# A sparse attention layer on one core: three pairs of tiles and a single one, turned by VectorE instead of TensorE, and slots cleared behind the sort

## The chip, the cores and the metric

The kernel runs on one core of a Trainium2 chip. The metric is the device time of one execution in microseconds. The engines are TensorE (PE, with its weight loads as PEld), VectorE (DVE), ScalarE (ACT), GpSimd (POOL) and SyncE (SP, which here only issues DMAs). GpSimd issues the indirect DMAs: gathers and scatters by a list of row numbers.

## The reference

```python
# x: (2708, 1024) f32; adj: (2708, 2708) f32 of zeros and ones, about 0.15% ones; W_q, W_k, W_v: (1024, 1024)
h = maximum(layernorm(x), 0)
q, k, v = h @ W_q.T + b_q, h @ W_k.T + b_k, h @ W_v.T + b_v
z = (q @ k.T) / sqrt(1024) * adj
z = where(z == 0, -10000, z)
out = x + relu(softmax(z, axis=1) @ v)
```

## The kernel before

A row of `adj` has a handful of ones, so the kernel never forms the full `z`. It finds each row's neighbours (at most 16), sorts the rows by their number of neighbours, and from then on works on 22 tiles of 128 sorted rows. `W_q` and `W_k` are multiplied into one matrix, so a score is a product of a transformed row `q` with a neighbour's row of `h`; and the weighted sum over neighbours' rows of `h` (the row `u`) is taken before `W_v` is applied. So there are two large products, each over 21 tiles or so: `q` from `h`, and the output `o` from `u`.

**Units.** The loop `for n, unit in enumerate(units)` (L1225) runs over 20 units: ten q pairs, (0,1) to (18,19), and ten o pairs in the order in which the attention finishes tiles; the last one is (16,9), and tile 8 comes alone behind them (`alone`). A unit multiplies a pair of tiles (256 rows) by a 1024x1024 matrix by Strassen's scheme in Winograd's form (`multiply`, L1044): seven block products instead of eight, each of four 128x512 steps in fp32, in banks `ps0`, `ps1` and `psy`. Between them `after(0)` to `after(6)` emit what other engines do meanwhile. The unit `FIRST` = 4 is pair (8,9), and `FIRST + 1` is the sixth, (10,11).

**Operands.** TensorE needs the tiles transposed. `blocks` (L711) makes the operands of the next unit: `a11`, `a12` from the first tile, `a22`, `s3` from the second, and their sums `s1` to `s4`. There are two ways. Either TensorE turns a tile in eight transposes of 128x128 (`half_turned`, L415; results in `pt`, copied by ScalarE, L718), or the tile arrives so that VectorE's transpose of 32x32 blocks suffices (`faces`, L705): ScalarE copies `u` with its columns in another order into `v` (L944), `v` is stored in `u_dram`, and SP loads it back by quarter rows (`by_quarters`, L700). A tile of the second kind stands in `faced_tiles`. Which tiles of o pairs are such is decided in `sums` when `u` is complete, by how far ahead of its unit that is:

```python
if now < [unit - 2, 2] and unit <= len(q_pairs) + 4:
    faced_tiles.add(t)
```

Of the q pairs none was such: the first eight tiles are taken as they come, the others are gathered whole from `h_dram` by GpSimd (`gather`, L612, tiles `qr_...`).

**The sort.** It is in two halves. Tiles 8 to 21 are sorted first, their table being stored in `tab_dram1` and loaded back. Tiles 0 to 7 (`EARLY`) are sorted in unit 4: VectorE finds the last keys, TensorE counts them (`ps_in`, `ps_all`, L678 and L680), VectorE makes the positions `pos_i` (L689), GpSimd puts the rows to `tab_dram0` in eight indirect DMAs (L626) and loads the table. Behind that it gathers `pq_6` and the first slots `g0` on, and the attention's stream begins.

**The attention.** Eleven slots `g0` to `g10` of 128x1024 (and two in `M`) hold neighbours' rows. Per slot VectorE makes a score (L863) and later a weighted addition to `u` (L923). This stream is advanced by `advance(share)` beside the products, 20.9 us a unit, less 2.3 us for each faced tile that VectorE has to turn. VectorE's order is as written (`manual_schedule`) from unit 4 on; the other engines' order is made by a scheduler. The slots are cleared once before the stream: eight on VectorE in front of the sort (L1254), three on GpSimd behind the counts (L1304).

**Outputs.** When an o pair is done, ScalarE applies relu to `y`, GpSimd adds rows of `x` by an indirect DMA that accumulates (`add_x`, L1109) and scatters `y` to the output (`scatter`, L808), each scatter standing behind the next add (`send`, L1168). The last pair goes through `ends` (L1140), the single tile through L1355 to L1371.

Of the kernel before, what the change touches and what calls it, by code (L numbers as in the profile page):

```python
# [10 lines left out]
FT = mybir.dt.float32  # L11
# [54 lines left out]
def tile_preln_masked_attention(  # L66
# [93 lines left out]
    pos_i = const.tile([P, NT], U32, name="pos_i")  # L160
    rows_i = whole[:, 0:NT]
# [488 lines left out]

    sorting, entered, sorted_at = [], [], []
# [267 lines left out]
    def sums(t):  # L919
# [20 lines left out]
        if now < [unit - 2, 2] and unit <= len(q_pairs) + 4:  # L940
            faced_tiles.add(t)
        if t in faced_tiles:
# [168 lines left out]
    def o_results(ta, tb):  # L1111
# [12 lines left out]
        def c12(Z, u2):  # L1124
# [5 lines left out]
            send(add_x(ya, ta))  # L1130
            sent.append((ya, ta))

        def c21(Y):
            nc.scalar.activation(yb[:, lo], Y, AF.Relu)  # L1134
            send(add_x(yb, tb))
            sent.append((yb, tb))
# [29 lines left out]
    sent = []  # L1166

    def send(behind):  # L1168

        while sent:  # L1170
            y, t = sent.pop(0)
            with tc.issue_after(behind.ins):
                scatter(y, t, P)

    def tail(t):
        n = tiles[t][1]
        y = work.tile([P, D], FT, tag="q", name=f"y_{t}", bufs=4)
        nc.sync.dma_start(y[:n], tail_dram.to_broadcast([n, D]))
        add_x(y, t, n)
        scatter(y, t, n)  # L1180
# [44 lines left out]
    for n, unit in enumerate(units):  # L1225
# [7 lines left out]
        share = 20.9 / 7  # L1233
# [5 lines left out]
        def after(i):  # L1239
            now[1] = i  # L1240
            if (n, i) in steps_ahead:
                follow(steps_ahead[n, i])
            if (n, i) == (2, 5):
                owe(8)
                owe(9)
                rows_of[FIRST] = load_rows(units[FIRST])
                owe(10)
                owe(6)
                owe(7)
                rows_of[FIRST + 1] = load_rows(units[FIRST + 1])  # L1250
                pooled.close()
            if (n, i) == (FIRST, 1):
                for g in slots[:HIGH - 3]:
                    nc.vector.memset(g, 0.0)  # L1254
# [23 lines left out]
            if nxt is not None:  # L1278

                if i == (3 if n == 0 else 4 if turn else 0):  # L1280
                    ops_of[n + 1] = blocks(*rows_of[n + 1], nc.gpsimd if n + 1 < FIRST - 1 else None)
                    with tc.issue_after(products[-1].ins) if n + 1 == FIRST else nullcontext():
# [18 lines left out]
            if (n, i) == (3, 5):  # L1301
                for s in range(8, HIGH):
                    for c in range(0, D, D // 4):
                        clear = nc.gpsimd.memset(slots[s][:, c:c + D // 4], 0.0)  # L1304
                        tc.add_manual_dep(clear.ins, counted_at[-1].ins.name,
                                          mybir.DependencyInfo(mybir.DependencyClass.Sync, mybir.DependencyReason.DATA),
                                          reason="not beside the counts")
            if i == 3 and units[n - 1][0] == "o" and NT - 2 in units[n - 1][1:]:
                tail(NT - 1)
            if nxt is None and i == 1:  # L1310
                while alone not in done:
                    advance(1.0)
                r, = load_rows(("o", alone))
                single["turned"] = turned(r, "alone")
# [240 lines left out]
```

## Time and profile before

| | |
|---|---|
| time, median of 3 runs | 639.91 us (639.73 to 640.34) |
| time of the profiled execution | 639.94 us |
| its span, first to last instruction | 638.1 us |
| granted TensorE clock, mean | 0.997 |
| busy: PE / DVE / ACT / POOL | 98% / 82% / 44% / 56% of the span |
| transposes on TensorE, L415 | 273 ns each |

A row of a group reads: line, engine, operation, output<-input, shape and count, then busy time in us, mean ns of one, and the idle time in front of them with what ended it. A row of a timeline reads: start and length in us, engine, line, operation, and in brackets the idle time in front and what ended it. A DMA row gives the size and the median time from issue to landing.

### The profile page before, as it was taken

Reading aid. Unit: us, or ns where it says so; the run is one execution under the profiler, and the core shown is the slowest. Engines: PE = TensorE matmul, PEld = TensorE weight load, DVE = VectorE, ACT = ScalarE, POOL = GpSimd, SP = SyncE. Lnnn points to the kernel's source line nnn. Section 1 sums busy time; section 2 is a strip of 40 time slices with the busy share of each in tenths; the row PEclk is TensorE's granted clock in tenths of the full one; section 3 lists DMA queues with packets and bytes.
Section 4 is the critical chain, followed back from the end, with each engine's and each line's share of the span. In section 5 each row is a group of like instructions: output and inputs, shape, how many; then the busy total and the mean of one; then the engine's idle time right before and its main releaser. Section 6 shows DMA issues by size and latency. Waiting matters only on the chain.

```text
span 638.1 us, 6156 instructions
## 1 busy us (share of the span) xinstructions
PE 627.8 (98%) x1651; PEld 317.9 (50%) x1651; DVE 522.4 (82%) x1016; ACT 283.6 (44%) x423; POOL 360.2 (56%) x383
## 2 busy tenths in 40 slices
PE   9999999999999999999999999999999999999994
PEld 5777766444444444444444444444444444444441
DVE  5999888997997625999888999999999889989121
ACT  3538985849667533424342144343342432333200
POOL 2639960885768357565651663476466878633311
PEclk9999999999999999999999999999999999999998
DMA  8999997598796439996798998999999999853631
GB/s 335 407 362 321 342 351 286 200 323 330 255 379 231 171 95 317 327 323 223 233 299 289 290 414 222 295 344 311 363 382 325 325 290 291 266 145 77 187 119 50
DMA packets 60192, 176.96 MB, mean 277 GB/s; under 512 B 9799, under 2 KB 15255, under 8 KB 59512
## 3 DMA queue, kind: packets, MB, share of 16 engines
q0 software_dynamic: 25136, 78.41, 39.4%
q1 hardware_dynamic: 29514, 78.61, 35.0%
q10 hardware_dynamic: 5502, 19.48, 7.8%
q8 instruction: 15, 0.25, 0.2%
q14 instruction: 25, 0.20, 0.1%
HBM read 145.65 MB, written 40.74 MB: 292 GB/s over the span
## 4 chain that ended last, share of the span: by engine, by line
PE 90%; issue 4%; POOL 2%; DMA 2%; DVE 1%; POOLq 0%; ACT 0%; ACTq 0%; DVEq 0%
PE ps L1010 40%; PE psy L1010 29%; PE ps_y L476 6%; PE ps_x L476 4%; PE ps_z L476 4%; PE pt L415 4%; POOL g L610 2%; DMA v_dram<-u 1%; DMA M<-h_dram,tab 1%; PE ps_y L511 1%; DVE junk L863 0%; PE ps_h L1218 0%; PE ps_v L594 0%; DVE u L923 0%; DVE s L722 0%
## 5 line engine op out<-in xcount | busy, mean ns | idle before, releaser
L610 POOL DMA_INDIRECT g<-h_dram,tab x94 | 120.2, 1278 | 79.9 <-DVE u L923 30.0
L1010 PE MATMUL psy<-wlow,s 128*128 128x512 f32 x320 | 144.0, 592 | 0.0
L1010 PE MATMUL ps<-M,a 128*128 128x512 f32 x320 | 144.0, 593 | 0.0
L863 DVE SCALAR_TENSOR_TENSOR junk<-g,pq 128x1024 uint8<-128x1024 f32 x93 | 113.8, 1224 | 13.4 <-DMA g<-h_dram,tab 10.4
L1010 PEld LDWEIGHTS ps<-M,a 128*128 128x128 f32 x320 | 59.7, 190 | 70.4 <-issue 69.1
L923 DVE SCALAR_TENSOR_TENSOR u<-g,coef,u 128x1024 f32<-128x1024 f32 x69 | 88.4, 1281 | 7.0 <-ACT u L912 5.8
L1010 PEld LDWEIGHTS psy<-wlow,s 128*128 128x128 f32 x320 | 59.6, 190 | 69.2 <-issue 69.0
L389 DVE FIND_INDEX8 at<-ones,adj 128x8 uint32<-128x685 f32 (+1 forms) x88 | 74.5, 864 | 0.0
L1010 PE MATMUL ps<-wlow,s 128*128 128x512 f32 x160 | 72.0, 593 | 0.4 <-DVE s L722 0.4
L1010 PE MATMUL ps<-M,s 128*128 128x512 f32 x160 | 72.1, 592 | 0.0
L1010 PE MATMUL psy<-wlow,a 128*128 128x512 f32 x160 | 72.0, 593 | 0.0
L368 ACT ACTIVATE sized<-adj 128x2708 uint8<-128x2708 f32 (+1 forms) x22 | 54.3, 2467 | 7.4 <-DMA adj<-in_adj_dram 6.1
L298 POOL TENSOR_TENSOR hsum<-hsum,x 128x256 f32<-128x256 f32 (+1 forms) x56 | 38.6, 732 | 26.2 <-DVE wlow L444 22.5
L1109 POOL DMA_INDIRECT y<-in_x_dram,tab x19 | 34.2, 1798 | 28.9 <-ACT y L1134 12.1
L1010 PEld LDWEIGHTS ps<-wlow,s 128*128 128x128 f32 x160 | 30.3, 190 | 38.9 <-issue 38.5
L1010 PEld LDWEIGHTS psy<-wlow,a 128*128 128x128 f32 x160 | 30.3, 190 | 38.5 <-issue 37.3
L1010 PEld LDWEIGHTS ps<-M,s 128*128 128x128 f32 x160 | 30.3, 190 | 38.1 <-issue 37.4
L808 POOL DMA_INDIRECT out_dram<-y,tab x21 | 27.4, 1306 | 32.0 <-DMA y<-in_x_dram,tab 15.8
L912 ACT ACTIVATE u<-g,coef 128x1024 f32<-128x1024 f32 x18 | 20.7, 1149 | 35.8 <-DVE coef L911 35.6
L276 ACT ACTIVATE x<-x,r 128x1024 f32<-128x1024 f32 (+1 forms) x22 | 25.9, 1232 | 6.6 <-POOL r L266 6.6
L722 DVE TENSOR_TENSOR s<-a,pt 128x512 f32<-128x512 f32 x30 | 19.2, 681 | 10.9 <-ACT a L718 10.9
L476 PE MATMUL ps_y<-wlow 128*128 128x512 f32 x64 | 27.6, 592 | 0.0
(251 smaller groups left out, 843.3 us busy)
## 6 DMA issues: line engine op xcount, KB each, us to landing
adj<-in_adj_dram SPq DMA_DIRECT2D x21, 1354.0 KB, 11.5
x<-in_x_dram SPq DMA_DIRECT2D x21, 512.0 KB, 8.2
h_dram<-x ACTq DMA_DIRECT2D x21, 512.0 KB, 7.4
q_late<-q SPq DMA_DIRECT2D x12, 512.0 KB, 5.1
pq<-q_late SPq DMA_DIRECT2D x12, 512.0 KB, 6.6
u_dram<-v ACTq DMA_DIRECT2D x10, 512.0 KB, 6.4
or<-u_dram SPq DMA_DIRECT2D x40, 128.0 KB, 7.0
M<-in_wv_dram SPq DMA_DIRECT2D x4, 1024.0 KB, 8.4
```

Of the source, the lines that this page charges most:

```text
L276: nc.scalar.activation(xs[i][:n], xs[i][:n], AF.Relu, bias=r[:n, 4, i:i + 1], scale=r[:n, 3, i:i + 1])
L298: small.append(nc.gpsimd.tensor_add(hsum[:n, cols], hsum[:n, cols], xt[:n, cols]))
L368: nc.scalar.activation(sized[:n], a[:n, :, :PW], AF.Abs, accum_out=total[:n, t:t + 1])
L389: nc.vector.max_index(at[:n, k - first_k, g, :], ones[:n, 0:8], a[:n, g, :])
L415: nc.tensor.transpose(pt[:, c, :], xt[:, k * P:(k + 1) * P], ident)
L476: mm = nc.tensor.matmul(bank, a_tile(o + H * a[0], a[1], i), b(o), start=first and o == 0, stop=(o == H - 1), skip_group_check=True)
L610: return nc.gpsimd.indirect_dma_start(out=dst, out_offset=None, in_=src, in_offset=off, bounds_check=N - 1, oob_is_err=False)
L808: to = nc.gpsimd.indirect_dma_start(out=out, out_offset=bass.IndirectOffsetOnAxis(ap=ptab.bitcast(U32)[:n, t, SLOTS:SLOTS + 1], axis=0), i ...
L863: chained(lambda: nc.vector.scalar_tensor_tensor(junk, g_of[t][s], 1.0, tq[t], op0=ALU.mult, op1=ALU.mult, accum_out=zall[:, t, s:s + 1]))
L923: chained(lambda: nc.vector.scalar_tensor_tensor(u, g_of[t][s], coef[:, s:s + 1], u, op0=ALU.mult, op1=ALU.add))
L1010: mm = nc.tensor.matmul(bank, a[:, c, :], b[:, c, :], start=False, stop=(c == 3), skip_group_check=True)
L1109: return nc.gpsimd.indirect_dma_start(out=y[:n], out_offset=None, in_=x, in_offset=off, compute_op=ALU.add)
```

## The change

Five tiles more are turned by VectorE. For the sixth q pair (10,11), unit 5, GpSimd makes a list of quarter rows: `load_parts` loads the pair's row numbers from `tab_dram1` in four small DMAs into `part_i`, one operation turns them into numbers of quarter rows (4 x row + quarter), and `gather_parts` gathers each tile in four indirect DMAs of 128x256. The tiles of the last o pair (16 and 9) and the single tile 8 become faced tiles: `v`, a store, four quarter loads, transposes on VectorE (tile 8 in one of 128x1024). The eight slots that VectorE clears are cleared behind the sort, in three groups; the three on GpSimd behind the puts. An add of `x` is issued some steps later than its tile is done, and a scatter one add later still. From unit 15 on `share` is 21.5 us.

```diff
+    def load_parts(t):
+        src = tab_dram[1][(t - EARLY) * P:(t - EARLY + 2) * P, SLOTS:SLOTS + 1].bitcast(U32).rearrange("(m r) w -> r m w", r=QP)
+        for a in range(QUADS):
+            load = nc.gpsimd.dma_start(part_i[a * QP:(a + 1) * QP, :].unsqueeze(2), src)
...
+    def gather_parts(dst, i):
+        faced.append(dst)
+        for g in range(QUADS):
+            off = bass.IndirectOffsetOnAxis(ap=part_i[:, i * QUADS + g:i * QUADS + g + 1], axis=0)
+            cols = slice(g * D // QUADS, (g + 1) * D // QUADS)
+            nc.gpsimd.indirect_dma_start(out=dst[:, cols], out_offset=None, in_offset=off,
+                                         in_=h_dram.rearrange("n (a w) -> (n a) w", a=QUADS))
...
-        if now < [unit - 2, 2] and unit <= len(q_pairs) + 4:
+        if now < [unit - 2, 2] and unit <= len(q_pairs) + 4 or unit >= len(units) - 1:
             faced_tiles.add(t)
...
-            send(add_x(ya, ta))
-            sent.append((ya, ta))
+            due.append((now[0], 5, ya, ta))
...
-            send(add_x(yb, tb))
-            sent.append((yb, tb))
+            due.append((now[0] + 1, 1, yb, tb))
...
+    def add_due():
+        while due and due[0][:2] <= tuple(now):
+            y, t = due.pop(0)[2:]
+            send(add_x(y, t), 1)
+            sent.append((y, t, P))
...
-        share = 20.9 / 7
+        share = (20.9 if n < len(units) - 5 else 21.5) / 7
...
                 rows_of[FIRST] = load_rows(units[FIRST])
+                load_parts(units[FIRST + 1][1])
                 owe(10)
                 owe(6)
                 owe(7)
-                rows_of[FIRST + 1] = load_rows(units[FIRST + 1])
+                nc.gpsimd.tensor_scalar(part_i, part_i, float(QUADS), quarter[:, 0:1], op0=ALU.mult, op1=ALU.add)
+                rows_of[FIRST + 1] = [row_tile(f"qr_{t}") for t in units[FIRST + 1][1:]]
+                for i, r in enumerate(rows_of[FIRST + 1]):
+                    gather_parts(r, i)
                 pooled.close()
-            if (n, i) == (FIRST, 1):
-                for g in slots[:HIGH - 3]:
-                    nc.vector.memset(g, 0.0)
+            if n == FIRST and i in (1, 4, 5):
+                for g in slots[:4] if i == 1 else slots[4:6] if i == 4 else slots[6:8]:
+                    with tc.issue_after(sorted_at[-1].ins):
+                        nc.vector.memset(g, 0.0)
...
-            if (n, i) == (3, 5):
+            if (n, i) == (3, 6):
                 for s in range(8, HIGH):
                     for c in range(0, D, D // 4):
+                        with tc.issue_after(entered[-1].ins):
+                            nc.gpsimd.memset(slots[s][:, c:c + D // 4], 0.0)
...
             if nxt is None and i == 1:
+                uT = work.tile([P, D], FT, tag="hT", name="T_alone", bufs=2).rearrange("p (c q) -> p c q", q=P)
+                faces(uT, single["rows"], 0, DC)
+                single["turned"] = uT
+            if n == len(units) - 2 and i == 6:
                 while alone not in done:
                     advance(1.0)
-                r, = load_rows(("o", alone))
-                single["turned"] = turned(r, "alone")
+                single["rows"], = load_rows(("o", alone))
```

The order on TensorE in unit 4, around the counting of the sort, before (the names without their numbers are the operands above; `qr_10` and `qr_11` are the sixth pair's tiles):

```order
L1010 MATMUL psy_1332<-wlow_171,a22_1237 128x512 x4
L1010 MATMUL psy_1482<-wlow_171,s2_1435 128x512
L678 LDWEIGHTS before_86
L678 MATMUL ps_in_1497<-sort_1454,before_86 128x144
L680 LDWEIGHTS ones_h_84
L680 MATMUL ps_all_1499<-sort_1454,ones_h_84 128x144
L415 MATMUL pt_1536<-ident_75,qr_10_1313 128x128 x4
L415 MATMUL pt_1543<-ident_75,qr_10_1313 128x128 x4
L1010 MATMUL psy_1482<-wlow_171,s2_1435 128x512 x3
L415 MATMUL pt_1564<-ident_75,qr_11_1315 128x128 x4
```

and the same place after the change:

```order
L1034 MATMUL psy_1358<-wlow_177,a22_1243 128x512 x4
L701 LDWEIGHTS before_86
L701 MATMUL ps_in_1512<-sort_1481,before_86 128x144
L703 LDWEIGHTS ones_h_84
L703 MATMUL ps_all_1514<-sort_1481,ones_h_84 128x144
L1034 MATMUL psy_1497<-wlow_177,s2_1462 128x512 x4
L1034 MATMUL ps0_1401<-M_154,a12_1424 128x512 x4
```

The transposes of `qr_10` and `qr_11` are gone, and the counting stands one step of `s2` sooner. In the same way the eight transposes of `u_16`, of `u_9` and of `u_8` go from units 18 and 19; nothing else moves on TensorE.

The order on GpSimd between the last q gathers and the attention's first gather, before (`hsum` are additions for another sum, `tab_dram0` takes the puts):

```order
L612 DMA qr_9_1299<-h_dram_63,tab_97 128x1024
L298 TENSOR_TENSOR hsum_73<-hsum_73,x_10_1123 128x256 x4
L298 TENSOR_TENSOR hsum_73<-hsum_73,x_6_944 128x256 x4
L298 TENSOR_TENSOR hsum_73<-hsum_73,x_7_946 128x256 x4
L612 DMA qr_10_1313<-h_dram_63,tab_97 128x1024
L612 DMA qr_11_1315<-h_dram_63,tab_97 128x1024
L612 DMA qr_12_1584<-h_dram_63,tab_97 128x1024
L612 DMA qr_13_1586<-h_dram_63,tab_97 128x1024
L1304 MEMSET g8_1411 128x256 x4
L1304 MEMSET g9_1412 128x256 x4
L1304 MEMSET g10_1413 128x256 x4
L626 DMA tab_dram0_70<-tab_97,pos_i_109 1024x18 x8
```

and after it:

```order
L659 DMA part_i_115<-tab_dram1_71 32x8x1 x4
L302 TENSOR_TENSOR hsum_73<-hsum_73,x_10_1129 128x256 x4
L302 TENSOR_TENSOR hsum_73<-hsum_73,x_6_950 128x256 x4
L302 TENSOR_TENSOR hsum_73<-hsum_73,x_7_952 128x256 x4
L1280 TENSOR_SCALAR part_i_115<-part_i_115,quarter_110 128x8
L671 DMA qr_10_1324<-h_dram_63,part_i_115 128x256 x4
L671 DMA qr_11_1325<-h_dram_63,part_i_115 128x256 x4
L616 DMA qr_12_1588<-h_dram_63,tab_97 128x1024
L616 DMA qr_13_1590<-h_dram_63,tab_97 128x1024
L630 DMA tab_dram0_70<-tab_97,pos_i_109 1024x18 x8
L1339 MEMSET g8_1438 128x256 x4
L1339 MEMSET g9_1439 128x256 x4
```

Ten DMAs and one small operation are added ahead of the puts, and the clears have moved behind them.

The order on VectorE behind the sort after the change (the rows without MEMSET and STREAM_TRANSPOSE stood there before as well, `pt` being read in place of `s3`):

```order
L712 COPY pos_i_109<-deg_98 128x8
L728 STREAM_TRANSPOSE a11_1563<-qr_10_1324 128x4x4x32
L728 STREAM_TRANSPOSE a12_1565<-qr_10_1324 128x4x4x32
L1288 MEMSET g0_1430 128x1024
L1288 MEMSET g1_1431 128x1024
L1288 MEMSET g2_1432 128x1024
L1288 MEMSET g3_1433 128x1024
L728 STREAM_TRANSPOSE a22_1577<-qr_11_1325 128x4x4x32
L728 STREAM_TRANSPOSE s3_1579<-qr_11_1325 128x4x4x32
L745 TENSOR_TENSOR s1_1581<-a22_1577,s3_1579 128x512
```

Four clears stand between the two tiles' transposes; the other four follow in pairs behind `q_8` and `q_9`.

29 lines of the change are left out of this document (17 added, 12 removed).

## The prediction

> **What bounds the kernel now.** I read the page first. Its busy times (us, share of the span, instructions):
>
> ```profile
> PE 627.8 (98%) x1651; PEld 317.9 (50%) x1651; DVE 522.4 (82%) x1016; ACT 283.6 (44%) x423; POOL 360.2 (56%) x383
> ```
>
> And its chain of the work that ended last, by engine:
>
> ```profile
> PE 90%; issue 4%; POOL 2%; DMA 2%; DVE 1%; POOLq 0%; ACT 0%; ACTq 0%; DVEq 0%
> ```
>
> TensorE is busy for 98% of the span and carries 90% of the chain. VectorE is the next busiest, at 82%. The view of TensorE's waits (line waited for, total us, times, longest) says how little could be gained by feeding it better:
>
> ```profile
> PE ps_y L511 <- POOL hsum L121: 1.2, 1, 1.2
> PE ps L1010 <- DVE s L722: 0.4, 1, 0.4
> ```
>
> The first is in the prologue, which the change leaves alone. The second is one hole in TensorE's timeline, in front of a product's `s1` block:
>
> ```profile
> 389.03 3.67 PE L1010 MATMUL ps<-wlow,s 128*128 128x512 f32 x8 [0.36 <-DVE s L722]
> ```
>
> So TensorE's own work sets the time, and work taken off it shortens the kernel one for one as long as VectorE still delivers its operands. The groups view (busy us, mean ns) and the pieces of the chain (start, us; the first and the last of the five that go) price the work that the change removes:
>
> ```profile
> L415 PE MATMUL pt<-ident,qr 128*128 128x128 f32 x96 | 12.4, 273 | 0.0
> ```
>
> ```profile
> 217.48 0.87 PE pt L415 x8
> ```
>
> ```profile
> 597.38 0.87 PE pt L415 x8
> ```
>
> One 128x128 transpose reads 273 ns, but they overlap; a tile's eight advance the chain by 0.87 us.
>
> **The change part by part.** *Transposes off TensorE.* Five tiles lose their eight: qr_10 and qr_11 (the first at 217.48), u_16 and u_9 (in the last pair but one's product), u_8 (597.38). Nothing takes their place on TensorE. 5 x 0.87 = 4.4 us; unrounded starts in the timeline give 4.37. By the fifth pair's end TensorE is 1.75 us ahead, by the last pair 3.5, by the single tile 4.37.
>
> *The same turns on VectorE.* The row of an operand that comes as quarter rows already:
>
> ```profile
> L705 DVE STREAM_TRANSPOSE a<-or 128x512 f32<-128x512 f32 x15 | 10.0, 694 | 1.0 <-DMA or<-u_dram 1.0
> ```
>
> A pair costs four transposes, 4 x 0.69 = 2.8 us, and its four additions stay. The single tile costs one of 128x1024, an estimate of 1.4 us from two of 128x512. That is 2.8 + 2.8 + 1.4 = 7.0 us more on VectorE. The Trainium skill, page "VectorE: DVE Perf Modes", section "Rules for kernel authors", speaks against this: a 128x128 transpose belongs on TensorE if it may land in PSUM. The trace agrees as far as the engine's own time goes (0.87 us a tile there, 1.4 on VectorE). It disagrees on what that is worth: one engine carries 90% of the chain, the other 1%. What the 7.0 us do where VectorE is the bound is a rival below.
>
> *The sixth pair's trip.* GpSimd now issues four small loads `part_i`, one small multiply-add, and eight quarter gathers in place of two whole ones. Its queue before, in the timeline:
>
> ```profile
> 194.48 8.25 POOL L298 TENSOR_TENSOR hsum<-hsum,x 128x256 f32<-128x256 f32 x12
> ...
> 206.62 0.93 POOL L612 DMA_INDIRECT qr<-h_dram,tab  x1 [0.30 <-issue]
> 217.37 3.13 POOL L1304 MEMSET g<- 128x256 f32 x12 [9.82 <-ACT q L1099]
> 220.68 1.02 POOL L626 DMA_INDIRECT tab_dram<-tab,pos_i  x1 [0.18 <-issue]
> ...
> 235.20 0.98 POOL L612 DMA_INDIRECT pq<-q_dram,tab  x1 [4.45 <-DMA tab<-tab_dram]
> ```
>
> ```profile
> L642 POOL DMA_DIRECT2D tab<-tab_dram x1 | 0.6, 601 | 0.0
> ...
> tab<-tab_dram POOLq DMA_DIRECT2D x1, 2.2 KB, 6.7
> ```
>
> The last `qr` gather ended at 207.55 and GpSimd then idled 9.82 us. Added: 4 x 0.60 = 2.4, some 0.2 for the multiply-add, and six more gathers of 0.94 + 0.30 = 7.4, together 10.0: it ends at 217.6. The small loads land about 6.7 us after their issue, behind which 8.25 us of additions stand anyway, so the gathers don't wait. A part of the queue that was idle is now full, with 2 us or so to spare. The tile is turned around 220 and first multiplied near 230, so a landing of some 7 us is covered.
>
> *The start of the stream.* VectorE's timeline around the sort, and where it later waits for TensorE:
>
> ```profile
> 219.82 0.17 DVE L689 CAST pos_i<-deg 128x8 uint32<-128x8 f32 x1
> 224.75 1.28 DVE L722 TENSOR_TENSOR s<-a,pt 128x512 f32<-128x512 f32 x2 [4.75 <-ACT a L718]
> ...
> 241.99 1.23 DVE L863 SCALAR_TENSOR_TENSOR junk<-g,pq 128x1024 uint8<-128x1024 f32 x1 [7.25 <-DMA g<-h_dram,tab]
> ...
> 333.57 0.69 DVE L1094 TENSOR_TENSOR q<-ps,u 128x512 f32<-128x512 f32 x1 [1.05 <-PE ps L1010]
> ```
>
> ```profile
> L1254 DVE MEMSET g<- 128x1024 f32 x8 | 7.3, 912 | 1.3 <-issue 1.1 <-DVE q L1094 0.2
> ```
>
> The eight clears (7.3 us) go behind the sort, into the idle stretch that holds the 4.75 and the 7.25 us above: 12.0 us, against 7.3 + 2.8 = 10.1 put there. The sort is then limited by TensorE's counting matmuls rather than by the clears, and `pos_i` comes 0 to 1 us sooner. GpSimd's three clears (3.13 us) go behind the eight puts, into the 4.45 us in which it waits for the sorted table. So the puts begin at 219.3 to 220.2 instead of 220.68, and the first score falls 0.5 to 1.4 us earlier. TensorE is 1.75 us earlier. The difference, 0.35 to 1.25 us, is what VectorE falls behind in relation to TensorE; the wait of 1.05 us at 333.57 shows that it still stood ahead by that much there. I take it that nothing is left of the difference, and that the hole at 389 stays at 0.4 us (0 to 1.2).
>
> *The end.* Each turned tile now takes a trip: a copy on ScalarE, a store, four quarter loads, the transposes. The rows: when `u_9` and `u_8` were complete on VectorE (the first and third), when TensorE wants the single tile, and the pieces of the trip.
>
> ```profile
> 558.72 2.60 DVE L923 SCALAR_TENSOR_TENSOR u<-g,coef,u 128x1024 f32<-128x1024 f32 x2
> ...
> 574.59 5.25 DVE L923 SCALAR_TENSOR_TENSOR u<-g,coef,u 128x1024 f32<-128x1024 f32 x4 [1.66 <-ACT u L912]
> ...
> 586.70 1.28 DVE L929 SCALAR_TENSOR_TENSOR u<-g,m,u 64x1024 f32<-64x1024 f32 x1
> ...
> 605.16 0.69 DVE L1146 SCALAR_TENSOR_TENSOR y<-ps,y 128x512 f32<-128x512 f32 x1 [13.22 <-PE ps L1010]
> ```
>
> ```profile
> 611.82 3.60 PE L1010 MATMUL ps<-M,T_alone 128*128 128x512 f32 x8
> ```
>
> ```profile
> L944 ACT COPY v<-u 128x1024 f32<-128x1024 f32 x10 | 10.5, 1046 | 22.6 <-DVE u L923 20.7 <-DMA g<-h_dram,tab 1.8
> ```
>
> ```profile
> u_dram<-v ACTq DMA_DIRECT2D x10, 512.0 KB, 6.4
> or<-u_dram SPq DMA_DIRECT2D x40, 128.0 KB, 7.0
> ```
>
> ```profile
> DMA to landing us min/median/max: 3.0/6.9/15.1
> ```
>
> `u_9` was complete at 561.3; with copy 1.05, store 6.4, issues 1.5 and load 7.0 it is back at 577.3, and VectorE reaches its transposes after three of the adds that began at 574.59 and two transposes more, near 579.5: about 2 us spare (both shift alike with the stream). The single tile is tighter. `u_8` was complete at 588.0. It comes 0.5 to 1.4 earlier with the stream and 2.5 later for the transposes ahead of it: 589.1 to 590.0. Copy 1.05, store 6.4, four quarter loads issued within some 1.5 us and landing in 7.0, transpose 1.4: 606.4 to 607.4 by the medians. Those medians come from a stretch of heavier traffic; with 5 us for each transfer it is 603.0 to 604.0. I take 605. TensorE wants it at 611.82 - 4.37 = 607.45. VectorE's 13.22 us of idleness takes the 1.4. So the cover is about 2.5 us, and may be nothing.
>
> *Adds and scatters later.* Each scatter now stands behind the next tile's add. No chain piece holds an output store before the end, the row buffers are seven, and GpSimd is busy for 56%; I cost it at nothing, up to 1 us where a ScalarE write waits for a landed scatter.
>
> **Sum.** 639.94 (the profiled execution) - 4.37 = 635.57; the median of the runs shown lies 0.03 lower, so 635.5. If the 0.4 us hole goes too, 635.1.
>
> **The rivals.** *Slower: tile 8's trip through DRAM is late.* It replaces transposes that read u_8 in place. If the quarter loads land in the 15.1 us that the slowest took, T_alone is ready at about 615, TensorE waits 7.5 us in front of its first T_alone product, and the time is 643.0. It costs anything from 607.45 on, and makes the kernel slower than before from 611.82 on, which takes both transfers at 18 us together instead of 13.4. For it: a serial chain of copy, store, loads and transpose within 18 us, at the least forgiving place. Against: traffic is thinning out there. Chance 0.18 of a stall of any size, most of it 0.5 to 3 us (636 to 638.5); 0.04 of it above 639.94 + 0.2%.
>
> *The stream starts late.* GpSimd's indirect issues take 0.94 us in the quiet stretch quoted above, but over the stream:
>
> ```profile
> L610 POOL DMA_INDIRECT g<-h_dram,tab x94 | 120.2, 1278 | 79.9 <-DVE u L923 30.0 <-ACT u L912 25.2 <-issue 18.3
> ```
>
> At 1.28 the ten gathers take 3.4 us more, the puts start at about 221 to 221.5, the first score shifts to 242.5 where TensorE is 1.75 earlier, and VectorE is 2.2 us behind it; less the 1.05 us that it waited there, the hole at 389 grows by 1.2, and by 2 if `s1` of the next pair is late as well: 636.7 to 637.5. The Trainium skill, page "SBUF — State Buffer", section "SBUF: two separate sides", has a cause: VectorE's two-port operations keep GpSimd from writing descriptors. The quiet gather of 0.93 us at 206.62 stands in the stretch in question, with VectorE at work beside it, so I give this case 0.14.
>
> *VectorE becomes the bound.* It is 82% busy on the whole. If its 7.0 us came on the path whole, the time would be 639.94 - 4.37 + 7.0 = 642.6. The Trainium skill's rule on transposes, quoted above, points to this case. Against it: 12 us of waits at the sort and 13 us at the end have room for all three turns. 0.04.
>
> *The transposes were hidden anyway,* and the time stays at 639.9. The chain runs through all five pieces and TensorE shows no wait behind them: 0.02.
>
> **How the numbers follow.** The forecast has the remaining 0.62. About 0.2% (1.3 us) is what a measurement of this kernel can tell from no change. Faster by more: 0.62, 0.11 of the late tile, 0.12 of the late stream, 0.85. Within: 0.03 + 0.01 + 0.02 = 0.06. Slower: 0.04 + 0.01 + 0.04 = 0.09. The range begins at 634.9, the filled hole with its spread, and reaches to 638.3, which takes in the late stream and most stalls of the late tile.
>
> **What would show it.** Right: 40 fewer matmuls in the groups on TensorE, its busy time near 623.4; L415 on no chain piece in the three places; puts starting near 220 and a first score near 241; no wait on T_alone. Wrong: a wait of TensorE for the transpose of `or_8` (late tile); puts later than 221 and larger waits for `s` from 389 on (late stream); VectorE without idle time at the sort or at 592 to 605 (bound moved).

## The result, and the profile after

The changed kernel takes 7087.17 us (median of 6 runs, 7085.40 to 7093.04); the kernel before takes 640.12 us beside it (6 runs, 639.63 to 642.51). That is 11.07 times as long, with an interval of 11.055 to 11.082. The profiled execution took 7085.67 us.

The first lines of the page of after, its two largest groups, and TensorE's largest waits:

```profile
span 7083.9 us, 25332 instructions
PE 4431.3 (63%) x8515; PEld 1830.2 (26%) x8515; DVE 1235.9 (17%) x2766; ACT 351.0 (5%) x478; POOL 367.8 (5%) x394
```

```profile
L1527 PE MATMUL g_u<-g_hk,g_pT 128*128 128x512 f32 (+1 forms) x1936 | 1646.3, 998 | 1471.8 <-DMA g_hk<-h_dram 1471.8
L1508 PE MATMUL g_ps<-hT_all,g_qT 128*128 128x512 f32 (+1 forms) x2112 | 814.3, 545 | 0.0
```

```profile
PE g_u L1527 <- DMA g_hk<-h_dram: 1471.8, 462, 3.5
PE g_q L1489 <- DMA g_m<-m_dram: 704.3, 176, 4.9
```

TensorE has 8515 matmuls where it had 1651. The added ones write tiles named `g_...`, at lines from 1426 on, of which the trace of before has none. They belong to a second, general way of computing the layer: dense attention over all rows, in the block behind `with tc.If(some > 0)` (L1412). It is there for inputs that the sparse way can't hold, and `some` is a flag that the kernel computes. TensorE's timeline around that point, and the windows to either side of it (us; busy time and count of PE, PEld, DVE, ACT, POOL; granted clock; DMA share; GB/s):

```profile
608.34 3.60 PE L1034 MATMUL ps<-M,T_alone 128*128 128x512 f32 x8
...
615.20 0.28 PE L1380 MATMUL ps_f<-many,ones 128*128 128x1 f32 x2
615.34 3.68 PE L1034 MATMUL ps<-wlow,T_alone 128*128 128x512 f32 x8
618.86 7.03 PE L1034 MATMUL ps<-M,T_alone 128*128 128x512 f32 x16
635.56 2.07 PE L1426 MATMUL g_pm<-gk,gq 128*128 128x512 f32 x2 [9.67 <-DMA gk<-in_wk_dram]
```

```profile
0.00:633.00 633.00, 623.92 (x1611) 313.92 (x1611) 530.44 (x1039) 283.28 (x418) 367.81 (x394) 1.00 0.85 285
633.00:7084.00 6451.00, 3807.35 (x6904) 1516.28 (x6904) 705.43 (x1727) 67.72 (x60) 0.00 (x0) 0.71 0.19 67
```

The kernel runs as the prediction describes it up to 625.9 us, with 1651 - 40 = 1611 matmuls. The sum `ps_f` at 615.20 carries the flag, and then the general way runs for 6451 us, 91% of the span. TensorE is busy for 59% of that, and its largest waits are for loads; the granted clock is 0.71.

**Why the flag is set.** VectorE searches each tile of `adj` for its neighbours' columns, in four instructions a tile (`found`). The groups of before and of after:

```profile
L389 DVE FIND_INDEX8 at<-ones,adj 128x8 uint32<-128x685 f32 x84 | 71.1, 865 | 0.0
```

```profile
L393 DVE FIND_INDEX8 at<-ones,adj 128x8 uint32<-128x685 f32 x80 | 67.8, 865 | 0.0
```

Four are missing: eight of two tiles are lost, and the four of a third are made twice. The order on VectorE shows where, in unit 2 behind step 5. (There the searches are called MAX_INDEX. `adj_158`, `adj_160` and `adj_162` are three buffers that are used in turn; after's name for the third is `adj_168`.) Before:

```
L1091 TENSOR_TENSOR q_1191<-psy,p_1174 128x512
L389 MAX_INDEX at<-ones,adj_158 128x8 x4
L389 MAX_INDEX at<-ones,adj_160 128x8 x4
L389 MAX_INDEX at<-ones,adj_162 128x8 x4
```

After:

```
L1115 TENSOR_TENSOR q_1197<-psy,p_1180 128x512
L393 MAX_INDEX at<-ones,adj_168 128x8 x4
L406 TENSOR_TENSOR cand<-first,at 128x128
L407 TENSOR_SCALAR cand<-at,cand 128x128
L410 MAX keys<-cand 128x8
...
L393 MAX_INDEX at<-ones,adj_168 128x8 x4
```

The searches in the first two buffers (`adj_158` and `adj_160` before) went. In their place the search of "f17" in the third (`adj_168`), which had been made already, stands again with the listing of its batch; the last row is the next search in that buffer, "f20", which before is the last row as well. The steps come from a table that `after(i)` reads at its end:

```python
(2, 1): "f17", (2, 2): "p16", (2, 3): "p17 a8 k8 z", (2, 4): "p18", (2, 5): "f18 f19", (2, 6): "p19 f20 p20",
...
            if (n, i) in steps_at:
                follow(steps_at[n, i])
```

The change put `for i, r in enumerate(rows_of[FIRST + 1]):` into the same function, on the branch that step (2,5) takes. Its `i` is the step number's `i`. The loop leaves it at 1, so the lookup finds (2,1), "f17", and not "f18 f19". These two are tiles 4 and 5 (tiles 8 to 21 are searched first). They are never searched, so in their rows the number of neighbours found differs from the number counted. `bad` says so (`nc.vector.tensor_tensor(bad, bad, total, op=ALU.not_equal)`, L1305), goes into `cap` (L1373) and so into the flag.

### The profile page after: what moved, and what is told of

Its sections match the earlier page's. It is cut to its first block, busy times and chain, and to the rows that moved or that the text cites. A ratio compares the mean times of both kernels' runs of the same rounds, so it can differ in the third digit from the quotient of the medians.

```text
span 7083.9 us, 25332 instructions
## 1 busy us (share of the span) xinstructions
PE 4431.3 (63%) x8515; PEld 1830.2 (26%) x8515; DVE 1235.9 (17%) x2766; ACT 351.0 (5%) x478; POOL 367.8 (5%) x394
## 5 line engine op out<-in xcount | busy, mean ns | idle before, releaser
L1527 PE MATMUL g_u<-g_hk,g_pT 128*128 128x512 f32 (+1 forms) x1936 | 1646.3, 998 | 1471.8 <-DMA g_hk<-h_dram 1471.8
L1527 PEld LDWEIGHTS g_u<-g_hk,g_pT 128*128 128x128 f32 (+1 forms) x1936 | 503.7, 287 | 2542.6 <-DMA g_hk<-h_dram 1724.6
L1489 PE MATMUL g_q<-g_m,g_qT 128*128 128x512 f32 x704 | 651.1, 1080 | 704.3 <-DMA g_m<-m_dram 704.3
L1508 PE MATMUL g_ps<-hT_all,g_qT 128*128 128x512 f32 (+1 forms) x2112 | 814.3, 545 | 0.0
L1489 PEld LDWEIGHTS g_q<-g_m,g_qT 128*128 128x128 f32 x704 | 205.8, 323 | 1122.4 <-issue 766.4
L1508 PEld LDWEIGHTS g_ps<-hT_all,g_qT 128*128 128x128 f32 x2112 | 383.9, 193 | 410.4 <-issue 410.4
L1541 PE MATMUL g_po<-wv,g_qT 128*128 128x512 f32 x704 | 341.5, 641 | 0.0
L1541 PEld LDWEIGHTS g_po<-wv,g_qT 128*128 128x128 f32 x704 | 143.9, 212 | 154.7 <-issue 154.7
L1426 PE MATMUL g_pm<-gk,gq 128*128 128x512 f32 x256 | 112.8, 604 | 9.7 <-DMA gk<-in_wk_dram 9.7
L1521 DVE COPY g_pT<-g_pp 128x128 f32<-128x128 f32 x484 | 105.4, 286 | 52.6 <-PE g_pp L1520 52.6
```

The lines of the kernel that those rows point to most:

```text
L1426: nc.tensor.matmul(ps, weights_q[o].rearrange("o (p c) -> o c p", c=DC)[:, c, :], weights_k[o][:, h * NB:(h + 1) * NB], start=(o == 0), st ...
L1489: nc.tensor.matmul(aq[h], qT[:, c, :], mc[:, h * NB:(h + 1) * NB], start=(c == 0), stop=(c == DC - 1))
L1508: nc.tensor.matmul(ps[:, :w], qT[:, c, :], hT[:, c, b0:b0 + w], start=(c == 0), stop=(c == DC - 1))
L1521: nc.vector.tensor_copy(pT[:kn, kc, :], pt[:kn, 0, :])
L1527: nc.tensor.matmul(au[h], pT[:kn, kc, :], hk[:kn, h * NB:(h + 1) * NB], start=(kc == 0), stop=(kc == NT - 1))
L1541: nc.tensor.matmul(ps, qT[:, c, :], wv_sb[h][:, c, :], start=(c == 0), stop=(c == DC - 1))
```

## The experiments on the cause

**The name alone.** The changed kernel with another name for the loop's variable:

```diff
-                for i, r in enumerate(rows_of[FIRST + 1]):
-                    gather_parts(r, i)
+                for m, r in enumerate(rows_of[FIRST + 1]):
+                    gather_parts(r, m)
```

> The changed kernel with one name changed: the loop over the two tiles of the sixth pair counts m instead of i, so that step 5 of unit 2 is still step 5 behind it. Theory A (the loop overwrote the step's number, step 5 did step 1's work again, tiles 4 and 5 were never searched, and the count of found neighbours sent the kernel through its general path): the general path is not taken and the time is 636.4 us, from the first T_alone product of the changed kernel's trace, 3.48 us earlier than before; between 635.5 and 637.0. Theory B (the clears behind the sort leave a slot uncleared): still near 7087. Theory C (the sixth pair's rows are gathered wrongly, their scores are out of range): still near 7087. The sixth pair's q differ from the reference's here: its quarters hold 256 neighbouring columns, where the blocks of the transposes want columns 128 apart.

It took 645.01 us (641.13 to 646.17), 0.9975 of the kernel before in the same job (0.9942 to 1.0007; before took 646.55 there). The searches are 84 again:

```profile
L393 DVE FIND_INDEX8 at<-ones,adj 128x8 uint32<-128x685 f32 x84 | 71.1, 867 | 0.0
```

So the general way is gone with the name. The time isn't the 636.4 expected; that is taken up below.

**The name in the kernel before.** One line, behind the loading of the sixth pair's rows, and nothing else of the change:

```diff
                 rows_of[FIRST + 1] = load_rows(units[FIRST + 1])
+                i = 1
```

> The kernel before with one line more, i = 1, at the place where the change has its loop; nothing else of the change is in it. Theory A: the general path is taken and the time is 7087 to 7100 us, with eight searches of a quarter row fewer for tiles 4 and 5 and four more for the tile searched at step 1. Theories B and C: 640 us, since neither the clears nor the sixth pair are touched.

```profile
span 7126.6 us, 25356 instructions
```

```profile
L389 DVE FIND_INDEX8 at<-ones,adj 128x8 uint32<-128x685 f32 x80 | 67.8, 868 | 0.0
```

One run: 7128.5 us. The kernel before falls to 80 searches as well and takes the general way, without any quarter gather, turn or later add.

**The count's part in the flag.** The changed kernel without one addition:

```diff
-        nc.vector.tensor_add(cap, cap, bad)
```

> The changed kernel as it is, with the overwritten index, but the comparison of found neighbours with the counted ones left out of the flag (one addition of 128x22 less). It leaves out the neighbours of tiles 4 and 5, and the test that finds that. Theory A: the flag stays zero and the time is 636.4 us. Theories B and C (another term of the flag): 7087.

One run: 643.82 us, span 642.1. The searches are still missing (80), and the general way doesn't run; the kernel leaves out the neighbours of tiles 4 and 5. The three runs close the chain: name, lost searches, unequal count, flag, general way.

## The experiments on the change itself

With the name mended, the change brings nothing that can be measured. Its parts were therefore tried apart, always against the kernel before in the same job. (Before took 640.12 us beside the changed kernel, 646.55, 643.47 and 646.28 us in the three jobs of experiments. Its first gather of a q tile began at 192.12 us in the prediction's trace and at 197.89 in the trace below, so runs are compared within a job. The three jobs ran on three chips, numbers 9, 11 and 12, so that what differs from job to job may differ from chip to chip.) A trace is of one run, which need not be near the median: 638.94 and 638.90 us for the kernel with the sixth pair on TensorE (medians 640.06 and 639.83), 646.06 for before (643.47), 649.20 for the end alone (644.59), 644.60 for the clears alone (643.52).

**The sixth pair left with TensorE.** The renamed kernel, with the sixth pair gathered whole and turned by TensorE as before; the clears, the end and the later adds stay:

```diff
-                load_parts(units[FIRST + 1][1])
...
-                nc.gpsimd.tensor_scalar(part_i, part_i, float(QUADS), quarter[:, 0:1], op0=ALU.mult, op1=ALU.add)
-                rows_of[FIRST + 1] = [row_tile(f"qr_{t}") for t in units[FIRST + 1][1:]]
-                for m, r in enumerate(rows_of[FIRST + 1]):
-                    gather_parts(r, m)
+                rows_of[FIRST + 1] = load_rows(units[FIRST + 1])
...
-                    with tc.issue_after((products if n + 1 == FIRST else sorted_at)[-1].ins) if n in (FIRST - 1, FIRST) else nullcontext():
+                    with tc.issue_after(products[-1].ins) if n + 1 == FIRST else nullcontext():
```

> As e1_rename, but the sixth pair is gathered whole and turned by TensorE as before; clears, last pair, single tile, adds and scatters as in the change. If the transposes count one for one: 24 of 40 gone, 2.62 us, 637.3 us, and e1_rename is 1.7 us below it. If VectorE's start sets the gain of the fifth pair (stream late): e1_rename is at most 1 us below it. If the new wait of TensorE for the sort (0.7 us in the changed kernel's trace) comes from the clears' new order, it is here too and the time is 638.0.

It took 640.06 us (638.94 to 643.27), 0.9904 of before (0.9877 to 0.9932), and 4.95 us less than the renamed kernel beside it. GpSimd's timelines show where they differ. The renamed kernel first (first q gather, last one, first put), then this one:

```profile
198.15 1.07 POOL L616 DMA_INDIRECT qr<-h_dram,tab  x1 [7.65 <-PE ps L1033]
...
224.35 0.93 POOL L616 DMA_INDIRECT qr<-h_dram,tab  x1 [0.30 <-issue]
225.59 1.04 POOL L630 DMA_INDIRECT tab_dram<-tab,pos_i  x1 [0.30 <-issue]
```

```profile
197.45 1.07 POOL L616 DMA_INDIRECT qr<-h_dram,tab  x1 [7.17 <-PE ps L1033]
...
212.17 0.94 POOL L616 DMA_INDIRECT qr<-h_dram,tab  x1 [0.30 <-issue]
220.93 1.01 POOL L630 DMA_INDIRECT tab_dram<-tab,pos_i  x1 [7.82 <-DVE pos_i L712]
```

In the renamed kernel the positions were ready at 221.2:

```profile
221.05 0.17 DVE L712 CAST pos_i<-deg 128x8 uint32<-128x8 f32 x1
```

but the puts began at 225.59, with no idle time ahead of them: GpSimd was still busy with the last quarter rows and, behind them, the next pair's two gathers. With whole rows it stood idle for 7.82 us. The first score of the attention came at 248.70 us there and at 242.47 here:

```profile
248.70 1.23 DVE L886 SCALAR_TENSOR_TENSOR junk<-g,pq 128x1024 uint8<-128x1024 f32 x1 [4.52 <-DMA g<-h_dram,tab]
```

```profile
242.47 1.23 DVE L886 SCALAR_TENSOR_TENSOR junk<-g,pq 128x1024 uint8<-128x1024 f32 x1 [5.21 <-DMA g<-h_dram,tab]
```

Of these 6.23 us the later puts are 4.66. Most of the rest lies in the gather of `pq`, which took 2.34 us in the renamed kernel, beside clears of VectorE (239.34 to 244), and 0.99 here:

```profile
240.39 2.34 POOL L616 DMA_INDIRECT pq<-q_dram,tab  x1 [1.44 <-DMA tab<-tab_dram]
```

```profile
235.57 0.99 POOL L616 DMA_INDIRECT pq<-q_dram,tab  x1 [1.38 <-DMA tab<-tab_dram]
```

These clears were late because VectorE had waited 6.58 us for a `q` at 238.49, where the profile names no engine as the cause. VectorE's order is fixed, and so the late stream holds up what stands behind it. The rows of the renamed kernel:

```profile
371.39 2.60 DVE L946 SCALAR_TENSOR_TENSOR u<-g,coef,u 128x1024 f32<-128x1024 f32 x2
373.90 0.68 DVE L1114 TENSOR_TENSOR q<-psy,p 128x512 f32<-128x512 f32 x1
```

```profile
374.64 5.40 PE L1033 MATMUL psy<-wlow,a 128*128 128x512 f32 x8 [3.89 <-DVE q L1114]
```

and of this one:

```profile
368.55 0.68 DVE L1114 TENSOR_TENSOR q<-psy,p 128x512 f32<-128x512 f32 x1
```

```profile
369.29 3.70 PE L1033 MATMUL psy<-wlow,a 128*128 128x512 f32 x8
```

The same result of the product is read out of `psy` 5.35 us later, behind two weighted additions of the attention, and TensorE waits 3.89 us for the bank. The wait is not the whole price. The eight matmuls behind it take 5.40 us for 3.70, since for 3.4 us the granted clock is 0.50 (window, PE busy and count, granted clock, DMA share, GB/s; renamed kernel):

```profile
371.90:375.30 3.40, 0.66 (x2) 1.00 1.02 418
375.30:378.70 3.40, 3.40 (x6) 0.50 1.02 417
378.70:382.10 3.40, 3.40 (x9) 1.00 1.02 408
```

**Both again, and a trace of before beside them.**

> The change with the index mended, again, for where the fifth pair's gain went in the first job (645.0 us, 5.0 above e4 with 1.75 us less work on TensorE). Theory S (stream late: the eight quarter gathers and four small loads stand ahead of the puts, and any delay of the first q gather goes through them to the first score): puts start at first q gather + 27.4 us in both jobs; if that gather starts at 192, puts at 220 and a time of 636.4; if at 198, puts at 225.6 and 641 to 646. Theory V (VectorE's own added work is the bound): the waits for q and s near 375 and 389 are of 3 us or more wherever the puts start.

> As e1 with the sixth pair turned by TensorE as before. Theory S: hardly touched by the start of the q gathers, since GpSimd waits 7.8 us for the positions ahead of the puts: 637.3 to 640 in either case, so that e1 is 1 us faster where the gather starts at 192, and 3 to 5 us slower where it starts at 198. Theory V: e1 is slower in both.

> The kernel before, for its trace beside the runs of this job. If the first job's 646.55 us came from late transfers in the prologue, its trace shows either 640 us with GpSimd's first q gather at 192 (as in the first trace), or some 645 us with that gather at 197 or later.

The renamed kernel took 644.92 us, 1.0009 of before (0.9984 to 1.0035); with the sixth pair on TensorE it was 639.83 us, 0.9946 (0.9925 to 0.9966). The distance is 5.1 us, as in the first job. In the second traces the first score comes at 247.04 and 242.47, and TensorE waits 3.0 us for `q` in the renamed kernel and not at all for it in the other. But the puts of the renamed kernel begin at 224.17 there, and the positions were ready only at 223.13: the gathers run 1.0 us past them and not 4.4. The positions themselves came 2.5 us later than in the other kernel (220.61); TensorE, which counts for them, had run at a granted clock of 0.50 from 204.0 to 207.4. So the 5 us are measured twice, and how they divide between the gathers ahead of the puts and what follows from them differs from run to run.

The trace of before shows why it is slower here than in the prediction's trace, and so leaves more to gain than three tiles on TensorE (2.6 us by the prediction's price):

```profile
197.89 1.07 POOL L612 DMA_INDIRECT qr<-h_dram,tab  x1 [6.13 <-PE ps L1010]
...
223.47 1.02 POOL L626 DMA_INDIRECT tab_dram<-tab,pos_i  x1 [0.18 <-issue]
```

```profile
203.64 1.06 PE L415 MATMUL pt<-ident,qr 128*128 128x128 f32 x8 [2.46 <-DMA qr<-h_dram,tab]
...
372.63 5.40 PE L1010 MATMUL psy<-wlow,a 128*128 128x512 f32 x8 [1.94 <-DVE q L1091]
```

Where the gathers start at 198, TensorE waits 2.46 us for the first gathered tile. The stream starts late too (first score at 244.47 for 241.99), and TensorE waits 1.94 us for `q`; the trace of the prediction shows neither wait. Behind the second the granted clock is 0.50 for 3.4 us, and TensorE is busy 1.7 us longer on the whole (629.5 for 627.8). The three add up to the 6.1 us by which the span is longer (644.2 for 638.1). The start of the stream is not all that makes `q` late: between first score and `q`, VectorE waits 7.93 us for an operand at 256.25, where it waited 3.70 in the prediction's trace, and the profile names no engine for it. The first of the two waits, 1.1 to 2.5 us, is in every trace of the three jobs whose kernel skips the general way, whatever way the sixth pair takes.

**The end alone.** The kernel before, with only the last pair and tile 8 turned by VectorE:

```diff
-        if now < [unit - 2, 2] and unit <= len(q_pairs) + 4:
+        if now < [unit - 2, 2] and unit <= len(q_pairs) + 4 or unit >= len(units) - 1:
...
+                faces(uT, single["rows"], 0, DC)
+                single["turned"] = uT
...
```

> The kernel before with only the last pair and the single tile turned by VectorE; clears, adds, scatters, sixth pair and share as before. If the end's 24 transposes alone count: 2.62 us below before, the same as e4 within 0.5 us. If the later adds and scatters, the clears or the share of 21.5 us are needed for that: it is 1 us or more above e4.

644.59 us, 1.0007 (0.9981 to 1.0033): no gain from 24 matmuls fewer.

```profile
619.84 3.70 PE L1010 MATMUL ps<-M,T_alone 128*128 128x512 f32 x8 [1.07 <-DVE T_alone L705]
```

TensorE waits for the single tile's trip, and 0.8 us more for `p` in the last unit. The rival named "tile 8's trip" is seen here, at 1.07 us.

**The clears alone.** The kernel before, with the two groups of clears moved as in the change:

```diff
-            if (n, i) == (FIRST, 1):
-                for g in slots[:HIGH - 3]:
-                    nc.vector.memset(g, 0.0)
+            if n == FIRST and i in (1, 4, 5):
+                for g in slots[:4] if i == 1 else slots[4:6] if i == 4 else slots[6:8]:
+                    with tc.issue_after(sorted_at[-1].ins):
+                        nc.vector.memset(g, 0.0)
...
-            if (n, i) == (3, 5):
+            if (n, i) == (3, 6):
...
+                        with tc.issue_after(entered[-1].ins):
+                            nc.gpsimd.memset(slots[s][:, c:c + D // 4], 0.0)
```

> The kernel before with the clears moved behind the sort and behind the puts, and nothing else. Theory S (the first put decides): the first put goes from 223.5 (trace of before in the job before) to 220.9, the wait of 1.9 us for q near 373 goes, and the time is 641 to 642, 2 to 3 us below before. Theory T (TensorE's transposes alone count): no change, 643.5.

643.52 us, 0.995 (0.9917 to 0.9983), 2.8 us less. TensorE's wait of 1.94 us for `q` is gone from its waits; GpSimd stood idle 10.27 us before the puts:

```profile
223.69 1.01 POOL L626 DMA_INDIRECT tab_dram<-tab,pos_i  x1 [10.27 <-DVE pos_i L689]
```

But the reason that was expected, puts 2.6 us sooner, is not what the trace shows. The positions came late in this run, the puts began at 223.69 (223.47 in the trace of before) and the first score at 245.53 (244.47). TensorE was later there as well, by 1.45 us near 293, having run at a granted clock of 0.50 from 203.7 to 207.1, and that by itself shortens a wait for VectorE. So the gain of the clears stands by its interval, and its cause is not shown.

**Clears and end together.** The two edits above in one kernel:

> The clears of e10 and the end of e5 together: 40 percent of the change, without the sixth pair, the later adds and scatters and the larger share. Theory S: 639.8, as e4. If the later adds, scatters or the share carry a part of e4's gain: above 640.5, with a wait for T_alone or p in the last unit as in e5's trace (1.1 and 0.8 us).

```profile
PE psy L1010 <- DVE q L1091: 2.4, 1, 2.4
...
PE ps L1010 <- DVE T_alone L705: 0.9, 1, 0.9
```

644.85 us, 0.9965 (0.9931 to 0.9999). The end added nothing to the clears that these runs can tell; its single tile is late again. The wait for `q` is back at 2.4 us, although the puts (221.89) and the first score (243.45) are sooner than with the clears alone; VectorE waited 9.21 us for an operand at 256.46 here and 6.31 there. So the start of the stream alone doesn't decide this wait.

**The adds as before.** The kernel with the sixth pair on TensorE, its adds and scatters put back where they stood:

```diff
-            due.append((now[0], 5, ya, ta))
+            send(add_x(ya, ta))
+            sent.append((ya, ta))
...
```

> e4 with adds and scatters where they were before. If they matter only off the path: 639.8, as e4. If the scatter ahead of the next add held up ScalarE or GpSimd: 0.5 to 2 us above e4, with waits in the o units.

642.23 us, 0.9938 (0.9899 to 0.9977): that is 4.05 us less than before beside it, against 6.5 and 3.6 with the later adds. So the runs don't tell the two apart. It differs from the kernel with clears and end together by the share from unit 15 on (and a small constant that nothing reads). The store of `v` for tile 8, its transpose and the product, in this kernel and in the second trace of the one with the later adds:

```profile
597.44 0.33 ACTq L969 DMA_DIRECT2D u_dram<-v  x1
```

```profile
613.01 1.25 DVE L728 STREAM_TRANSPOSE T_alone<-or 128x1024 f32<-128x1024 f32 x1 [15.61 <-DMA or<-u_dram]
```

```profile
614.31 3.70 PE L1033 MATMUL ps<-M,T_alone 128*128 128x512 f32 x8 [1.46 <-DVE T_alone L728]
```

```profile
593.23 0.33 ACTq L969 DMA_DIRECT2D u_dram<-v  x1
```

```profile
605.58 1.25 DVE L728 STREAM_TRANSPOSE T_alone<-or 128x1024 f32<-128x1024 f32 x1 [12.38 <-DMA or<-u_dram]
```

From the store's issue to the transpose it is 15.57 us with the adds as before and 12.35 with the later ones; the store itself was issued 4.21 us later as well. The stalls of 0.9 to 1.5 us at the single tile appear in the three kernels with the old adds (this one and the two before it with the end turned), and in none of the seven traces of kernels with both the turned end and the later adds (after, the one without the count's part in the flag, the renamed kernel twice, the one with the sixth pair on TensorE twice, and the one below). The trip takes 13.8 to 15.6 us in the three and 11.6 to 12.4 in the seven. The trip's length is what makes the stall: TensorE came 14.2 to 15.4 us behind the store in the three, and with a trip of 12.4 us and a transpose of 1.25 us it would not have waited. That the adds' transfers lengthen the trip fits; the transfers were not timed one by one, and the two kernels' times come from different jobs.

**The next pair's gathers behind the puts.** The renamed kernel, with the gathers of `qr_12` and `qr_13` issued behind the puts:

```diff
-                    rows_of[n + 2] = load_rows(units[n + 2])
+                    with tc.issue_after(entered[-1].ins) if n == FIRST else nullcontext():
+                        rows_of[n + 2] = load_rows(units[n + 2])
```

> The change with the index mended, and the two gathers of qr_12 and qr_13 behind the puts instead of ahead of them (two of the ten that stand between the positions and the puts). As e1, the sixth pair's q differ. Theory S: the first put comes 2.5 us sooner than in e1 (about 222), the first score 1.3 us sooner (two gathers and three clears now fill more than the wait for the table), the wait near 373 shrinks by as much, and the time is 643. Theory V (VectorE's work is the bound): no change to e1, 645.

```profile
223.65 1.03 POOL L630 DMA_INDIRECT tab_dram<-tab,pos_i  x1 [1.20 <-issue]
```

644.49 us, 0.9963 (0.9933 to 0.9994). The puts begin 1.94 us sooner than in the renamed kernel's first trace, but the two gathers now stand between puts and stream, and the first score comes at 247.99 (248.70 and 247.04 in the renamed kernel's two traces). The issues are moved, not removed, and the stream starts as late. TensorE's wait for `q` is 2.3 us (3.9 and 3.0 there). The time lies between the 643 and the 645 us of the two theories, so this run doesn't decide between them.

The version with the sixth pair on TensorE has the lowest times: 0.9904 and 0.9946 of the kernel before in two jobs, 6.5 and 3.6 us. Next to the clears alone (0.995) and the adds as before (0.9938) that is no clear lead.

## Why the prediction was wrong

**The step that failed.** The prediction's step "The change part by part" priced what the diff says and what the order shows around the turns, and nothing for the rows of unit 2. There the order of VectorE had lost two searches and shown one twice. The order of the changed kernel says so before any run, and the prediction doesn't count its rows over the whole kernel: 84 searches of 128 rows before, 80 after. What the runs showed in its place is the general way, 6451 us. The rivals had a change whose gain was hidden ("The transposes were hidden anyway"), and none in which the edit does something else than it says, so nothing in the range of 634.9 to 638.3 stands for the general way.

**What the sum said of the rest.** The changed kernel's trace up to 625.9 us still tests its terms, under transfers as in the trace of before (first q gather at 192.35 against 192.12):

- *Transposes off TensorE.* Its busy time is 623.92 us ("near 623.4"), with 40 fewer in the groups: x80 of `qr` for x96, x32 of `u` for x56. TensorE reached the single tile's product at 608.34 for 611.82, 3.48 us sooner where 4.37 was expected. A new wait takes most of the rest; no trace with the name mended has it:

```profile
151.69 0.28 PE L701 MATMUL ps_in<-sort,before 128*128 128x252 bf16 x1 [0.67 <-DVE sort L689]
```

- *The start of the stream.* The puts began at 220.71 and the first score at 242.33, not at 219.3 to 220.2 and 240.6 to 241.5. The term "`pos_i` comes 0 to 1 us sooner" was worth nothing here. GpSimd waited for `pos_i`, with 2.08 us to spare, as the prediction had it ("2 us or so").

```profile
220.71 1.03 POOL L630 DMA_INDIRECT tab_dram<-tab,pos_i  x1 [2.08 <-DVE pos_i L712]
```

- *The end.* `T_alone` was ready at 602.87 + 1.25 = 604.1; the estimate was 605 and TensorE wanted it at 608.34. In this run the trip was covered by 4.2 us. The later adds, which the prediction costs at nothing, belong to this cover: with the adds as before the trip took 13.8 to 15.6 us (above), and here it took 11.9.

```profile
602.87 1.25 DVE L728 STREAM_TRANSPOSE T_alone<-or 128x1024 f32<-128x1024 f32 x1 [11.95 <-DMA or<-u_dram]
```

**The second step that failed.** Even with the name mended 635.5 was not reached in these jobs: 645.01 and 644.92 us, and no gain over the kernel before beside it (1.0009, 0.9984 to 1.0035). The prediction's cover, "with 2 us or so to spare" on GpSimd, was read from one trace in which the gathers start at 192. In the renamed kernel they start at 197 to 198, the two microseconds are used up, and the ten more DMAs that GpSimd issues run 4.4 us past the positions in one trace and 1.0 in the other. In the changed kernel's own trace, with the same DMAs and the gathers from 192.35, the cover holds, and TensorE has no wait for `q`. The rival "the stream starts late" has the right place and the right wait (VectorE behind, TensorE waiting for it), but another cause: it took the gathers to last 1.28 us each, and most of them last 0.95 to 1.07, near the old price; their start is what moved. It gave 636.7 to 637.5. In these jobs it is the case that holds, with a larger price: the sixth pair's new way costs 5 us net, the 1.75 us that it saves on TensorE already taken off. Two terms of that price are missing in the sum: the granted clock behind a wait, and the slower gather of `pq` beside VectorE's clears.

"VectorE becomes the bound" holds at that one place and not on the whole. Its four transposes of 0.69 us are not what made it late: behind them it stood waiting, 6.58 and 4.29 us in the renamed kernel's two traces, before the first score. The traces put the delay on the gathers of quarter rows ahead of the puts and on what followed from them; the one run meant to test that, with two gathers moved, left it undecided. The Trainium skill ("VectorE: DVE Perf Modes", "Rules for kernel authors") gives a 128x128 transpose to TensorE if the result may land in PSUM. For the sixth pair the runs agree with it, by these 5 us, for a reason that, as the traces have it, lies on GpSimd's queue.

**Open.** What the renamed kernel takes where the gathers start at 192 was not measured; its two traces have them at 198.15 and 197.40. The single tile's stall was not followed to a particular transfer. VectorE's waits of 4.29 to 9.21 us without a named engine, near 238 or 256, are unexplained. And the change leaves something out for tiles 10 and 11. VectorE's transposes need a tile whose columns were put into another order, as ScalarE does it for `v`; `gather_parts` takes 256 neighbouring columns of `h` at a time and puts nothing into order, so the `q` of these two tiles is not the reference's, in the changed kernel and in the renamed one. This is read from the code. Gathering pieces of 32 columns instead was not tried, so the 5 us are the price of a way that is not complete.

## What to carry to other kernels

Count the instructions of each kind, engine by engine, before and after a change, and account for every one that is lost or doubled; a "move" must leave the count alone. In a kernel with a guarded general way, one lost instruction upstream can turn into a factor of 11, so ask of every edit what it does to the guard's inputs. And a queue's spare time in one trace is spare only under that trace's transfers: a cover of 2 us on a queue whose start hangs on other work is not a cover until the spread of that start is known.

## What had not been expected of the hardware

The same program ran differently from one job to the next: the first gather of a q tile began at 192.12 us in one trace of the kernel before and at 197.89 in another, and its median time went from 640.12 to 646.55 us. Not only the landings differ. The stores of `h`, on whose landing the gather waits in the first trace, were issued from 180.19 us on there and from 184.42 on in the other, after waits of ScalarE (2.42 and 4.09 us) that the first doesn't have; why is open.

A short wait of TensorE can cost more than itself. Behind waits of 3.89 us (renamed kernel) and 1.94 us (the second trace of before) the granted clock was 0.50 for 3.4 us, which made the next eight matmuls 1.7 us longer; behind a wait of 2.37 us at the same place, with clears and end together, it stayed at 1.00. In the general way the granted clock was 0.71 while TensorE was busy for 59% of the time (3807 of 6451 us), against 1.00 at 99% (623.92 of 633 us) in the sparse part.
